# Strassen additions moved from VectorE into TensorE's accumulation, and more TensorE work during the list building, in a masked attention layer on one core

## The chip, the cores and the metric

The kernel runs on one core of a Trainium2 chip. The metric is the device time of one execution in microseconds. The kernel before takes 2042.49 us (median of three runs, 2041.43 to 2042.58). The profile below is of one execution with a span of 2041.5 us and a mean granted TensorE clock of 0.977.

The engines have short names: PE is TensorE (PEld its weight loads), DVE is VectorE, ACT is ScalarE, POOL is GpSimd, SP is SyncE. PSUM, where matmuls write, has eight banks of 128 x 512 float32; SBUF holds everything else.

## The reference

For x of shape (16, 1024, 512) and a sparse 0/1 matrix adj of shape (1024, 1024), with eight heads of 64 and float32 throughout:

```python
q = (x @ Wq + bq).reshape(b, n, H, HD)
k = (x @ Wk + bk).reshape(b, n, H, HD)
v = (x @ Wv + bv).reshape(b, n, H, HD)
scores = einsum('bqhd,bkhd->bhqk', q, k) / sqrt(HD) + (1.0 - adj) * -1e9
out = einsum('bhqk,bkhd->bqhd', softmax(scores), v).reshape(b, n, d)
return layernorm(x + out @ Wo + bo)
```

adj has few ones: the kernel works with a list of neighbours for each query instead of the full score matrix.

## The kernel before, in words

**Lists.** At the start the queries are sorted by their number of neighbours, and `edges(t)` makes, for each of eight tiles of 128 queries, columns of key rows: `OWN` columns with one key for each query of the tile (29 in all), and for the two tiles with the most neighbours `BLOCKS` shared columns (6 in all). So a batch of x has NB = 35 blocks, and 16 batches have 560. The lists are the same for all batches and are made once, mostly by DVE.

**Fronts.** For each batch the rows of x are transposed on PE (`transpose_x`) and multiplied by Wq (`product`, four accumulated matmuls of 128 x 512) and by Wk and Wv. The last two are done together for a pair of row tiles in `pair(b, j)`: the pair's 2 x 2 blocks (two row tiles by two halves of the depth) against the 2 x 2 blocks B11, B21 (Wk) and B12, B22 (Wv) are one Strassen-Winograd product with seven half-depth products where the plain one has eight. The combinations of the weights are T1 to T4, those of x are s1 to s4 (`combine`). Each half-depth product is a `unit` of two matmuls. The results go to `kv_rows` and `q_rows` in HBM. The very first pair is done plainly. Every float32 matmul of the program is two instructions in the trace.

With p1 = x00·B11 in bank x, the kernel before forms the outputs so:

- ACT copies p1 from bank x to an SBUF tile e (`out_e`, L679). PE then adds p2 onto bank x, and ACT copies that out as k of the first row tile (`out_k`, L583).
- DVE adds p6 (its own bank) and e into w (`out_w`, L682), p7 and w into g (`out_g`, L685), and p4 and g into k of the second row tile (`out_k1`, L689).
- p5 goes to bank z; DVE adds z and g into v of the second row tile (`out_v1`, L694). PE adds the last product onto z, and DVE adds z and w into v of the first row tile (`out_v0`, L698).

So there are five DVE additions of 128 x 512 for each of the 63 Strassen pairs.

**Blocks.** For block n, POOL gathers 128 rows of k and v (`gather`, L810), DVE multiplies by q (`products`, L827) and sums over each head (`scores`, L831), ACT takes the exponential (`exponentials`, L841), and the values are multiplied by it (`weigh`). This last can be done by ACT, as eight instructions of 128 x 64 (L851), or by DVE, as one of 128 x 512 (L855); `by_act(n)` chooses. The products are then added by DVE (`add_own`, L867) or, for the shared columns, by PE (`add_up`, L876 and L877). `normalise` divides, PE transposes (`poT`, L902), ACT copies (`oT`, L906), and `finish` does the output projection (`po`, four matmuls), the residual and the layer norm, and POOL scatters the rows out.

**Order.** The program's order is written by hand, and each engine runs its instructions in that order. A loop over steps n goes from -34 (`LEAD_IN`) past 560; a step works on several blocks in turn (scores of n + 4, exponentials of n + 3 and so on). In each step PE also gets units of fronts or of a finish until a `credit` is used up, which grows by `share` a step; a unit is booked at `PRODUCT` = 0.86 for one matmul of 512 columns. Before block 0 the share is `LEAD_SHARE`. At each batch's start the share is set from what is left to a goal. The goal depends on the batch alone, so whatever was done early is taken off the next share. `later(k, fn)` puts the copy that empties a bank k steps on. A Strassen unit may name a result that it needs; while the step that makes it has not been written yet, no further unit is put out.

**Banks.** Four PSUM banks are shared by everything that is emptied soon (`fill_psum`: projections, transposes, p4, p6, p7), x and z have one each, and two hold the sums of the shared columns. A bank can be written again when what is in it has been read.

Of the kernel before, what the change touches and what calls it, by code (L numbers as in the profile page):

```python
# [10 lines left out]
F32 = mybir.dt.float32  # L11
# [3 lines left out]
OP = mybir.AluOpType  # L15
# [9 lines left out]
OWN = (1, 2, 2, 3, 4, 5, 5, 7)  # L25
# [16 lines left out]
LEAD_IN = 34  # L42
# [3 lines left out]
SUM = 0.87  # L46
TRANSPOSE = 0.44
LEAD_SHARE = 3.45
LAST_SHARE = 3.0

P = 128
# [103 lines left out]
def kernel(  # L155
# [35 lines left out]
    nc = tc.nc  # L191
    B, N, D = x.shape
# [3 lines left out]
    HALF = N // 2  # L196
# [25 lines left out]
    with ExitStack() as main:  # L222
# [4 lines left out]
        dram = main.enter_context(tc.tile_pool(name="dram", bufs=1, space=bass.MemoryType.DRAM))  # L227

        def fill_psum(name):
            return psum.tile([P, HALF], F32, tag="fill", name=name, bufs=4)  # L230

        neg_half = one.tile([P, 1], F32, name="neg_half")
        nc.gpsimd.memset(neg_half, -0.5)
# [106 lines left out]
        def later(k, fn):  # L340
            plan.setdefault(now[0] + k, []).append(fn)

        def later_last(k, fn):
            rest.setdefault(now[0] + k, []).append(fn)
# [219 lines left out]
        def pair(b, j):  # L564
# [25 lines left out]
            def send(i):  # L590
                kv = KV[b, tt[i]]
                later(1, lambda: nc.sync.dma_start(kv_rows[b % ROWS][ds(tt[i] * P, P), :], kv))
                R["sent"] = R.get("sent", 0) + 1
                if R["sent"] == 2:
                    later(1, add_v)
                    if j == NT // 2 - 1:
                        later(2, lambda: urgent.append(mean_pe))
# [57 lines left out]
            def a(i, h):  # L655
                return XT[b, tt[i]][:, ts(h, HD2)]

            def unit(bank, left, right, first, after, need):
                def pe():
                    if first:  # L660
                        R[bank] = fill_psum(f"p{bank}_{b}_{j}") if bank[0] == "p" else psum.tile(
                            [P, HALF], F32, tag=bank, name=f"{bank}_{b}_{j}", bufs=1
                        )
                    l = left()
                    for c in range(2):
                        nc.tensor.matmul(  # L666
                            R[bank], l[:, ts(c, P)], right[:, c, :], start=(first and c == 0), stop=(c == 1),
                            skip_group_check=True,
                        )
                    later(1, after)  # L670

                return [(2 * PRODUCT, pe, lambda: (need is None or need in R) and (b, j) in SX)]

            def temp(name):
                R[name] = work.tile([P, D], F32, tag=name, name=f"{name}_{b}_{j}", bufs=1)
                return R[name]

            def out_e():
                nc.scalar.copy(temp("e"), R["x"])  # L679

            def out_w():
                nc.vector.tensor_tensor(temp("w"), R["p6"], R["e"], op=OP.add)  # L682

            def out_g():
                nc.vector.tensor_tensor(temp("g"), R["p7"], R["w"], op=OP.add)  # L685

            def out_k1():
                kv = KV[b, tt[1]]
                nc.vector.tensor_tensor(kv[:, 0:D], R["p4"], R["g"], op=OP.add)  # L689
                send(1)  # L690
                later_last(1, lambda: norm(b, tt[1], 1, kv[:, 0:D]))

            def out_v1():
                nc.vector.tensor_tensor(new_kv(1)[:, D:], R["z"], R["g"], op=OP.add)  # L694
                R["v1"] = True

            def out_v0():
                nc.vector.tensor_tensor(KV[b, tt[0]][:, D:], R["z"], R["w"], op=OP.add)  # L698
# [2 lines left out]
            def s(i):  # L701
                return lambda: SX[b, j][i - 1]

            units = []
            units += unit("x", lambda: a(0, 0), B11, True, out_e, None)
            units += unit("p6", s(2), T2, True, out_w, None)
            units += q0
            units += unit("x", lambda: a(0, 1), B21, False, lambda: out_k(0, R["x"]), "e")
            units += unit("p7", s(3), T3, True, out_g, None)
            units += xt  # L710
            units += unit("z", s(1), T1, True, out_v1, None)
            units += q1
            units += unit("p4", lambda: a(1, 1), T4, True, out_k1, None)
            units += unit("z", s(4), B22, False, out_v0, "v1")
            return units

# [125 lines left out]

        def by_act(n):
            b, t, i = blocks[n]
            return 0 < i < OWN[t] or n % 2 == 0 or n < NB // 2

        def weigh(n):
            v, pv = KG.pop(n), PV[n]
# [108 lines left out]
        out_rows = {(b, t): out_views[b * NT + t].rearrange("b n d -> (b n) d") for b in range(B) for t in range(NT)}  # L957
        done, coming, spilled, gathered, fronts = [], [], [], [0], []

        total = len(blocks)  # L960
        prep = {}
        for t in range(NT):
# [5 lines left out]
        with tc.manual_schedule():  # L968
# [13 lines left out]
            while n < total or plan or rest or urgent or done or finishing or spilled:  # L982
                now[0] = n
                if n < 0:
                    share = LEAD_SHARE if n > -LEAD_IN else TRANSPOSE * 1.5
                elif n >= SPILL[0] // NT * NB + NB:

                    share = sum(u[0] for u in fronts) / max(fronts_end - n, 1) + NS * SUM / NB if fronts else LAST_SHARE
                elif n % NB == 0:

                    left = sum(u[0] for u in fronts)
                    goal = fronts_time - (n // NB + 2 + (EARLY + (FIRST if n < NB else 0)) / NB) * batch_time
                    share = (max(0.0, left - goal) + NT * NPAIR * PRODUCT + NS * SUM) / NB
                if 0 <= n + 3 < total:
                    exponentials(n + 3)
                if 0 <= n + 4 < total:
                    products(n + 4)
                while gathered[0] < min(n + (AHEAD if fronts else AHEAD_LAST) + 1, total) and blocks[gathered[0]][0] in set_up:
                    gather(gathered[0])
                    gathered[0] += 1  # L1000
                if 0 <= n + 1 < total and not by_act(n + 1):
                    weigh(n + 1)
                if 0 <= n < total and blocks[n][2] < OWN[blocks[n][1]]:
                    add_own(n)
                if 0 <= n + 4 < total:
                    scores(n + 4)
                if 1 <= n <= total and (n == total or blocks[n][2] == 0):
                    normalise(*blocks[n - 1][:2])
                for fn in plan.pop(n, ()):
                    fn()  # L1010
                if 0 <= n + 2 < total and by_act(n + 2):
                    weigh(n + 2)
                for fn in rest.pop(n, ()):
                    fn()
                credit += share
                if 0 <= n < total and blocks[n][2] >= OWN[blocks[n][1]]:
                    add_up(n)
                    credit -= SUM
                for tile_done in done[:0 if fronts and len(done) < LAZY else 1 if fronts else 2] + coming:
                    if tile_done not in loaded and sum(b * NT + t not in SPILL for b, t in Y) < 5:  # L1020
                        load_y(*tile_done)
                coming[:] = [t for t in coming if t not in loaded]
                if spilled and not fronts and n > last_reload + 2 and sum(b * NT + t in SPILL for b, t in Y) < 3:
                    reload(*spilled.pop(0), reloads)
                    reloads, last_reload = reloads + 1, n
                first_unit = True
                while credit > 0 or urgent:
                    if urgent and not (first_unit and fronts):
                        urgent.pop(0)()
                        continue  # L1030
                    if not finishing and len(done) > (LAZY if fronts else 0) and n > loaded.get(done[0], n) + 1 and n > last_finish + 1:
                        finishing = finish(*done.pop(0))
                        last_finish = n
                    units = finishing or fronts
                    if not units:
                        if urgent:
                            urgent.pop(0)()
                            continue
                        break
                    cost, fn, ready = units[0]  # L1040
                    if ready and not ready():
                        if urgent:
                            urgent.pop(0)()
                            continue
                        break
                    del units[0]
                    fn()
                    credit -= cost
                    first_unit = False
                credit = min(credit, share)  # L1050
                preps += prep.pop(n, [])
                preps = [g for g in preps if next(g, True) is None]
                n += 1
# [34 lines left out]
```

## Time and profile before

| What | Value |
|---|---|
| Time, median of 3 | 2042.49 us |
| PE busy | 1917.2 us, 94% |
| DVE busy | 1801.0 us, 88% |
| ACT busy | 1684.6 us, 83% |
| POOL busy | 1302.5 us, 64% |
| DMA queue with the largest share | 59.8% of the 16 engines' span |

Busy time is the union of an engine's instructions. Matmuls overlap in the pipeline, so PE's share says when something was in it and not how densely it was fed. The groups of instructions give the line, the engine, the operation, its tiles and shapes, the count, the busy time and the mean of one; then the engine's idle time ahead of them and who ended most of it. The windows give each engine's busy time in a stretch of the span, the granted TensorE clock (1.00 is full) and the share of the DMA engines.

### The profile page before, as it was taken

The numbers are of one execution on the slowest core, as the hardware profiler recorded it, in microseconds if no ns is written. First come the engines' busy times: TensorE is split into PE (matmuls) and PEld (weight loads), VectorE is DVE, ScalarE is ACT, GpSimd is POOL, SyncE is SP. The second block draws the span as 40 slices with busy tenths as digits, with TensorE's granted clock in tenths as the row PEclk, the third lists the DMA queues.
The fourth block names the chain that finished last, engine by engine and source line by source line (L and its number), as shares of the span: only waits on it lengthen the run. The fifth ranks groups of instructions, "written<-read, shape, count | busy, mean of one in ns | idle before, by whom it ended". The sixth has DMA issues, their size and how long they took to land. (4 is left out here: it accounts for less than half of the span.)

```text
span 2041.5 us, 26505 instructions
## 1 busy us (share of the span) xinstructions
PE 1917.2 (94%) x5334; PEld 925.4 (45%) x5334; DVE 1801.0 (88%) x3675; ACT 1684.6 (83%) x7048; POOL 1302.5 (64%) x1224
## 2 busy tenths in 40 slices
PE   8979999899999999999999999999999999997565
PEld 4434454444545444444544444454544444443232
DVE  3798889889999989989999999989999999997684
ACT  4627879888897988889897989879798889987684
POOL 1432557757576666757676676758677675757884
PEclk9999999999999999999999999999999999999897
DMA  6565787878888787878888797888888799978773
GB/s 244 154 202 195 241 297 264 296 237 303 288 295 292 261 307 258 310 242 303 293 287 307 242 327 250 293 283 289 293 271 305 257 321 313 326 255 281 231 253 103
DMA packets 183657, 549.50 MB, mean 269 GB/s; under 512 B 30879, under 2 KB 30907, under 8 KB 183486
## 3 DMA queue, kind: packets, MB, share of 16 engines
q0 software_dynamic: 121632, 403.22, 59.8%
q1 hardware_dynamic: 59248, 139.53, 18.4%
q10 hardware_dynamic: 2606, 4.99, 0.7%
q14 instruction: 127, 1.04, 0.2%
q8 instruction: 44, 0.72, 0.1%
HBM read 435.44 MB, written 136.89 MB: 280 GB/s over the span
## 5 line engine op out<-in xcount | busy, mean ns | idle before, releaser
L810 POOL DMA_INDIRECT kvg<-kv_rows,key_row x560 | 634.9, 1134 | 468.1 <-ACT pv L841 145.1
L851 ACT ACTIVATE pv<-kvg,pv 128x64 f32<-128x64 f32 x3608 | 910.2, 342 | 0.0
L550 PE MATMUL pq<-wq,xT 128*128 128x512 f32 x1024 | 479.7, 599 | 0.2 <-DVE g L685 0.2
L550 PE MATMUL po<-wo,oT 128*128 128x512 f32 x944 | 439.0, 599 | 0.7 <-ACT oT L906 0.7
L831 DVE TENSOR_REDUCE s<-qk 128x8 f32<-128x512 f32 x560 | 381.0, 680 | 6.4
L827 DVE TENSOR_TENSOR qk<-qt,kvg 128x512 f32<-128x512 f32 x464 | 317.4, 684 | 5.9 <-DMA kvg<-kv_rows,key_row 5.8
L550 PEld LDWEIGHTS pq<-wq,xT 128*128 128x128 f32 x1024 | 193.8, 192 | 216.2 <-issue 197.4
L550 PEld LDWEIGHTS po<-wo,oT 128*128 128x128 f32 x944 | 176.5, 192 | 209.2 <-issue 191.8
L666 PE MATMUL x<-b,xT 128*128 128x512 f32 x504 | 239.1, 597 | 0.0
L666 PE MATMUL pp<-t,s 128*128 128x512 f32 x504 | 237.0, 592 | 0.4 <-DVE s L536 0.4
L867 DVE TENSOR_TENSOR pv<-pv,pv 128x520 f32<-128x520 f32 x336 | 233.1, 694 | 0.2 <-ACT pv L851 0.2
L841 ACT ACTIVATE pv<-s,absent 128x8 f32<-128x8 f32 x464 | 136.9, 296 | 85.1 <-DVE s L831 55.8
L767 POOL DMA_INDIRECT out_dram<-y,asked_row x128 | 151.0, 1180 | 35.5 <-issue 16.9
L725 POOL DMA_INDIRECT y<-in_x_dram,asked_row x128 | 143.0, 1117 | 38.9 <-issue 37.7
L562 ACT ACTIVATE sq<-q 128x128 f32<-128x128 f32 x512 | 151.1, 303 | 17.5 <-DVE q L577 17.1
L794 POOL DMA_INDIRECT qt<-q_rows,asked_row x128 | 140.4, 1097 | 38.9 <-issue 34.6
L562 ACT ACTIVATE sq<-kv 128x128 f32<-128x128 f32 x512 | 151.0, 302 | 0.1
L666 PEld LDWEIGHTS x<-b,xT 128*128 128x128 f32 x504 | 95.8, 191 | 116.6 <-issue 111.5
L666 PEld LDWEIGHTS pp<-t,s 128*128 128x128 f32 x504 | 94.8, 190 | 110.6 <-issue 99.2
L902 PE MATMUL poT<-ident,o 128*128 128x128 f32 x512 | 79.5, 279 | 50.2 <-DVE o L894 34.1
L666 PE MATMUL z<-b,s 128*128 128x512 f32 x252 | 120.1, 599 | 5.0 <-DVE kv L694 5.0
L804 POOL DMA_INDIRECT qg<-q_rows,query_row x96 | 106.9, 1114 | 27.8 <-issue 24.1
(168 smaller groups left out, 2816.1 us busy)
## 6 DMA issues: line engine op xcount, KB each, us to landing
kv_rows<-kv SPq DMA_DIRECT2D x128, 512.0 KB
x<-in_x_dram SPq DMA_DIRECT2D x128, 256.0 KB
q_rows<-q SPq DMA_DIRECT2D x128, 256.0 KB
kvg<-kv_rows,key_row POOLq DMA_INDIRECT x560, 5.8
adj<-in_adj_dram POOLq DMA_DIRECT2D x8, 512.0 KB, 12.7
spill<-oT SPq DMA_DIRECT2D x10, 256.0 KB
oTs<-spill SPq DMA_DIRECT2D x10, 256.0 KB
qt<-q_rows,asked_row POOLq DMA_INDIRECT x128, 5.0
```

The costliest lines, as they stand in the source:

```text
L550: nc.tensor.matmul(p, lhs()[:, ts(c, P)], w[:, c, :], start=(c == 0), stop=(c == NPAIR - 1))
L562: nc.scalar.activation(sq, s[:, ts(h, P)], AF.Square, accum_out=NRM[b][:, i, t, h:h + 1])
L666: nc.tensor.matmul(R[bank], l[:, ts(c, P)], right[:, c, :], start=(first and c == 0), stop=(c == 1), skip_group_check=True,)
L725: nc.gpsimd.indirect_dma_start(out=Y[b, t], out_offset=None, in_=x_rows, in_offset=bass.IndirectOffsetOnAxis(ap=asked_row[:, t:t + 1], axi ...
L767: nc.gpsimd.indirect_dma_start(out=out_rows[b, t], out_offset=bass.IndirectOffsetOnAxis(ap=asked_row[:, t:t + 1], axis=0), in_=y, in_offse ...
L794: nc.gpsimd.indirect_dma_start(out=QT[b, t], out_offset=None, in_=q_rows[b % ROWS], in_offset=bass.IndirectOffsetOnAxis(ap=asked_row[:, t: ...
L810: nc.gpsimd.indirect_dma_start(out=KG[n], out_offset=None, in_=kv_rows[b % ROWS], in_offset=bass.IndirectOffsetOnAxis(ap=key_row[:, g:g + ...
L827: nc.vector.tensor_tensor(QK[n], q, KG[n][:, 0:D], op=OP.mult)
L831: nc.vector.tensor_reduce(S[n], QK.pop(n).rearrange("p (h d) -> p h d", d=HD), axis=AX.X, op=OP.add)
L841: nc.scalar.activation(PV[n][:, D:], S.pop(n), AF.Exp, bias=bias)
L851: nc.scalar.activation(pv[:, ts(h, HD)], v[:, ds(D + h * HD, HD)], AF.Copy, scale=pv[:, D + h:D + h + 1])
L867: nc.vector.tensor_tensor(PV[b, t], PV[b, t], pv, op=OP.add)
```

## The change

Three of the five additions go to PE. ACT copies p1 from bank x into a third bank u (a PSUM bank of its own, taken from the shared ones, which are now three). PE adds p6 onto it, and ACT copies the sum out as w. PE adds p7 onto the same bank, and ACT copies that out as g. PE adds p4, and ACT copies that out as k of the second row tile. The two additions with z stay on DVE. So that a matmul can add onto what ACT wrote, one matmul writes bank u at the start.

The units are put in another order: z's first product comes ahead of the transposes of the next pair, and p7 and p4 each wait, in the writing of the program, for the copy out of u (p4 for the addition of g into v one step after that).

Every second of the eligible blocks that ACT weighed goes to DVE: `n % 2` becomes `n % 4`. And from step -15 to step -1, where the lists are made, the share of PE work rises from 3.45 to `LISTS_SHARE` = 4.6.

```diff
+LISTS_SHARE = 4.6
...
-            return psum.tile([P, HALF], F32, tag="fill", name=name, bufs=4)
+            return psum.tile([P, HALF], F32, tag="fill", name=name, bufs=3)
+
+        def chain_psum(name):
+            return psum.tile([P, HALF], F32, tag="u", name=name, bufs=1)
...
             def out_e():
-                nc.scalar.copy(temp("e"), R["x"])
+                R["u"] = chain_psum(f"u_{b}_{j}")
+                nc.scalar.copy(R["u"], R["x"])
 
             def out_w():
-                nc.vector.tensor_tensor(temp("w"), R["p6"], R["e"], op=OP.add)
+                R["w"] = work.tile([P, D], F32, tag="w", name=f"w_{b}_{j}", bufs=1)
+                nc.scalar.copy(R["w"], R["u"])
 
             def out_g():
-                nc.vector.tensor_tensor(temp("g"), R["p7"], R["w"], op=OP.add)
+                R["g"] = work.tile([P, D], F32, tag="g", name=f"g_{b}_{j}", bufs=1)
+                nc.scalar.copy(R["g"], R["u"])
+                later(1, out_v1)
...
-                nc.vector.tensor_tensor(kv[:, 0:D], R["p4"], R["g"], op=OP.add)
+                nc.scalar.copy(kv[:, 0:D], R["u"])
...
             units += unit("x", lambda: a(0, 0), B11, True, out_e, None)
-            units += unit("p6", s(2), T2, True, out_w, None)
             units += q0
-            units += unit("x", lambda: a(0, 1), B21, False, lambda: out_k(0, R["x"]), "e")
-            units += unit("p7", s(3), T3, True, out_g, None)
+            units += unit("u", s(2), T2, False, out_w, "u")
+            units += unit("x", lambda: a(0, 1), B21, False, lambda: out_k(0, R["x"]), "u")
+            units += unit("z", s(1), T1, True, None, None)
             units += xt
-            units += unit("z", s(1), T1, True, out_v1, None)
+            units += unit("u", s(3), T3, False, out_g, "w")
             units += q1
-            units += unit("p4", lambda: a(1, 1), T4, True, out_k1, None)
+            units += unit("u", lambda: a(1, 1), T4, False, out_k1, "v1")
             units += unit("z", s(4), B22, False, out_v0, "v1")
...
-            return 0 < i < OWN[t] or n % 2 == 0 or n < NB // 2
+            return 0 < i < OWN[t] or n % 4 == 0 or n < NB // 2
...
+        nc.tensor.matmul(chain_psum("u_first"), ident, place[:, 0:HALF], start=True, stop=True)
...
-                    share = LEAD_SHARE if n > -LEAD_IN else TRANSPOSE * 1.5
+                    share = LISTS_SHARE if n > -16 else LEAD_SHARE if n > -LEAD_IN else TRANSPOSE * 1.5
```

More of the change, by code (lines that the diff above doesn't have):

```diff
@@ L660, in pe @@
                     if first:
-                        R[bank] = fill_psum(f"p{bank}_{b}_{j}") if bank[0] == "p" else psum.tile(
-                            [P, HALF], F32, tag=bank, name=f"{bank}_{b}_{j}", bufs=1
-                        )
+                        R[bank] = psum.tile([P, HALF], F32, tag=bank, name=f"{bank}_{b}_{j}", bufs=1)
                     l = left()
@@ L669, in pe @@
                         )
-                    later(1, after)
+                    if after:
+                        later(1, after)
                 return [(2 * PRODUCT, pe, lambda: (need is None or need in R) and (b, j) in SX)]
-            def temp(name):
-                R[name] = work.tile([P, D], F32, tag=name, name=f"{name}_{b}_{j}", bufs=1)
-                return R[name]
             def out_e():
-                nc.scalar.copy(temp("e"), R["x"])
+                R["u"] = chain_psum(f"u_{b}_{j}")
+                nc.scalar.copy(R["u"], R["x"])
             def out_w():
-                nc.vector.tensor_tensor(temp("w"), R["p6"], R["e"], op=OP.add)
+                R["w"] = work.tile([P, D], F32, tag="w", name=f"w_{b}_{j}", bufs=1)
+                nc.scalar.copy(R["w"], R["u"])
             def out_g():
-                nc.vector.tensor_tensor(temp("g"), R["p7"], R["w"], op=OP.add)
-            def out_k1():
-                kv = KV[b, tt[1]]
-                nc.vector.tensor_tensor(kv[:, 0:D], R["p4"], R["g"], op=OP.add)
-                send(1)
-                later_last(1, lambda: norm(b, tt[1], 1, kv[:, 0:D]))
+                R["g"] = work.tile([P, D], F32, tag="g", name=f"g_{b}_{j}", bufs=1)
+                nc.scalar.copy(R["g"], R["u"])
+                later(1, out_v1)
             def out_v1():
@@ L695, in out_v1, with out_k1 @@
                 R["v1"] = True
+            def out_k1():
+                kv = KV[b, tt[1]]
+                nc.scalar.copy(kv[:, 0:D], R["u"])
+                send(1)
+                later_last(1, lambda: norm(b, tt[1], 1, kv[:, 0:D]))
             def out_v0():
```

## The prediction

> **What bounds the kernel now.** I read the totals first, then the 40 slices, then the windows of six stages, because the stages here have different limits. From the page, the totals and four rows of slices (51 us each):
>
> ```profile
> PE 1917.2 (94%) x5334; PEld 925.4 (45%) x5334; DVE 1801.0 (88%) x3675; ACT 1684.6 (83%) x7048; POOL 1302.5 (64%) x1224
> ...
> PE   8979999899999999999999999999999999997565
> ...
> DVE  3798889889999989989999999989999999997684
> ACT  4627879888897988889897989879798889987684
> ...
> PEclk9999999999999999999999999999999999999897
> ```
>
> Busy PE need not be dense PE. The PE timeline settles it; start, length, and how many matmuls:
>
> ```profile
> 1011.20 3.60 PE L550 MATMUL pq<-wq,xT 128*128 128x512 f32 x8
> 1014.63 1.88 PE L666 MATMUL x<-b,xT 128*128 128x512 f32 x4
> ```
>
> Eight matmuls take 1014.63 - 1011.20 = 3.43 us, 0.429 each from start to start. A batch needs 240 of them (8 tiles x 8 for q, 8 x 8 for the output projection, 4 pairs x 28), so 103.0 us. Add 64 transposes at 0.109 (7.0), 24 matmuls of the shared sums at 0.22 (5.3) and two for the mean (0.9): 116.2 us. The matmul of the mean (L610) stands at 606.8 in one batch and 723.3 in the next, 116.5 us apart. In the middle PE has no gap at all.
>
> The windows (PE, PEld, DVE, ACT, POOL, then clock, DMA share, GB/s):
>
> ```profile
> 90.00:180.00 90.00, 71.55 (x180) 32.66 (x179) 86.93 (x190) 35.87 (x168) 25.02 (x25) 0.91 0.54 178
> 180.00:285.00 105.00, 104.96 (x291) 49.49 (x291) 88.74 (x174) 87.68 (x386) 59.85 (x55) 1.00 0.77 261
> 315.00:375.00 60.00, 51.66 (x147) 23.72 (x146) 58.94 (x128) 58.32 (x239) 44.87 (x44) 1.00 0.84 284
> 450.00:1650.00 1200.00, 1198.78 (x3392) 582.50 (x3391) 1113.94 (x2263) 1060.62 (x4499) 823.28 (x755) 1.00 0.83 285
> 1695.00:1770.00 75.00, 71.25 (x204) 33.44 (x203) 74.23 (x134) 75.00 (x345) 46.90 (x38) 1.00 0.92 320
> 1860.00:2010.00 150.00, 93.57 (x226) 44.23 (x225) 114.80 (x278) 109.86 (x393) 119.44 (x123) 0.85 0.73 238
> ```
>
> The lists (90 to 180) are DVE's: 97% busy, with PE idle for 18 us and at a lower clock. The rest of batch 0 (180 to 285) is PE's. Batch 1 (315 to 375) is held by DVE at 98% and ACT at 97% together, since its PE share is small. The middle is PE's. Around 1695 to 1770 ACT never rests. In the tail POOL is 80% busy with gathers about 0.3 us apart and no other engine is above 77%.
>
> **What the skill says.** Trainium Kernel Development and Optimization, section Performance Expectations, calls matmul busy time a bad metric of nearness to the roofline and prefers the share of weight loads. The trace agrees on the first (busy 3.60 us for 3.43 of spacing); on the second it shows 45% PEld in a stretch without gaps, so I go by spacing. PSUM — Partial Sum Buffer, The four PSUM rules, says that a matmul without the starting flag adds onto what another engine wrote where an earlier matmul has set the bits: that is what the one matmul on u is for, and it means the three additions cost PE nothing; no run here shows it yet. TensorE: Matmul & The Clock Gate, Step-by-step: what each phase is for, says only weight loads are pulled ahead and matmuls stay in program order, so a matmul that waits for ACT holds all PE work. The waits of before agree: PE sat still in front of poT for DVE's o for 34.1 us while other units stood behind it.
>
> **The change, part by part.** The rows for it:
>
> ```profile
> L851 ACT ACTIVATE pv<-kvg,pv 128x64 f32<-128x64 f32 x3608 | 910.2, 342 | 0.0
> ...
> L855 DVE TENSOR_TENSOR pv<-kvg,pv 128x512 f32<-128x512 f32 x109 | 74.7, 686 | 0.0
> ...
> L685 DVE TENSOR_TENSOR g<-pp,w 128x512 f32<-128x512 f32 x63 | 43.2, 686 | 17.2 <-PE pp L666 16.8
> ...
> L679 ACT COPY e<-x 128x512 f32<-128x512 f32 x63 | 36.6, 581 | 77.8 <-PE x L666 77.8
> ```
>
> *PE.* Two instructions more, under 1 us, while PE waits for its first data. Its 5334 instructions stay, so the middle can't get shorter.
>
> *DVE and ACT.* Three additions fewer for each of 63 pairs: 189 x 0.685 = 129 us off DVE. Three copies more on ACT: 189 x 0.58 = 110 us. The copy into u goes to PSUM, which no row shows; the nearest row is the copy to SBUF at 0.581, and ScalarE: Activation LUTs, What ACT_TABLE_LOAD costs, prices an ACTIVATE without pointer operands at 186 + 0.833 x 512 = 612 ns (estimate). I take 0.58; the difference over 63 is 2 us. The rule n % 4 moves 56 blocks: 448 ACT instructions of 910.2 / 3608 = 0.252 us, so -113 us, and 56 x 0.686 = +38 us for DVE. Totals: DVE -91, ACT -3. A middle batch has DVE 5.8 us lighter and ACT level (12 x 0.58 = 7.0 against 3.5 x 2.02 = 7.1). All hidden behind PE there.
>
> *The share of the lists.* Fifteen steps get 1.15 more, 17.25 us of PE work, and the planner takes it off batch 0. A pair is 19.8 us of PE and costs DVE 7.9 us now (two q, five additions, four halves of s, two of the mean) and 5.85 after. The lists hold about 2.65 pairs: DVE -5.4 for the additions, +5.1 for the 0.87 pair moved in. So DVE's bound there stays 90 us, and PE's 71.6 rises to about 89 of 90, tight. Batch 0's PE falls from 105 to 88 us; DVE there comes to about 77 and ACT to about 80, so PE still ends last. Gain 17 us at most; I allow 3 us for a tight lists stretch where PE and DVE wait for each other: **-14**.
>
> *Batch 1*, held by DVE and ACT: 2.4 pairs x 2.05 off DVE, 3.5 x 0.69 on; ACT +4.2 and -7.1. Both about -3: **-3**. *1695 to 1770*, held by ACT, which is level: **-1**. *Tail*, held by POOL: **0**.
>
> *New waits in the middle.* In the built order of the changed program I looked at how much PE work lies between the matmul that an ACT or DVE instruction waits for and the matmul that waits for that instruction. Along the u chain it is 3.4 us at least from p1 to p6, 4.3 from p6 to p7 and 3.4 from p7 to p4, with medians of 6.4, 8.2 and 7.3. In the trace of before, ACT has emptied x into e 0.62 us after p1's end in the median, 2.9 in the slowest tenth, 3.15 at most. So the chain itself seldom stops PE. The three shared banks do: in nine batches the second transpose of xT at the batch's end needs the bank of poT, whose copy waits for the end of a po, and only 0.44 us of PE work lies between. In the old order no such distance is under 2.15 us. Copy 0.62 + lateness of ACT (mean 1.2 - 0.62) + 0.05 - 0.44 gives 0.8 us each. In eight batches a q product then waits for DVE's y 2.6 us after po ended; y is done after 2.2 us on average, so about 0.3. Together about 1 us a batch: **+9**; 4 if ACT is always early, 25 if the new copies, 12 a batch that each tie ACT to PE, eat ACT's 13 us of slack a batch (1200 - 1060.62 over 10.3 batches). Behind a late copy on ACT stand the exponentials and the weighing, and for those waits the shared sums on PE.
>
> Sum: -14 - 3 - 1 + 9 = -9, so 2042.5 - 9 = **2033.5 us**.
>
> **Rivals.** *More relief:* PE and DVE fit together in the lists (-18), batch 1 gains on both engines (-6), 1695 to 1770 is eased (-4), the bank waits are short (+2): 2016. For it speaks that DVE's lateness should fall with its load; against it that ACT, not DVE, never rests at 1700. *Evened out:* the bank waits cost 1.75 us a batch (+19) and lists and batch 1 give -18: 2043. For it speaks that y is over 4 us late in a tenth of cases. *Slower:* ACT becomes late. 24 synchronised copies a batch become 36, and PE loses 3.5 us a batch over 10.3 batches, +36 - 18: 2060. For it speaks ACT's 88% and that e already had to wait 77.8 us for PE, time that ACT can't use ahead; against it that ACT's total work doesn't rise.
>
> **How the numbers follow.** Likeliest case 0.53, more relief 0.16, evened out 0.15, slower 0.16. Faster by over 0.2% (below 2038.4) holds the first two: 0.69; same 0.15; slower 0.16. The range from 2013 to 2055 holds the first three cases and the near edge of the last.
>
> **What would show it.** Right: PE idle in 90 to 180 falls from 18 us to under 8, block 35's scores (281.0 before) come 10 to 17 us sooner, ACT has 7048 - 259 and DVE 3675 - 133 instructions, and the middle shows a PE gap of about 1 us once a batch in front of pxT with ACT's oT as its end. Wrong: a middle batch of over 118.5 us with PE waiting on u for ACT (the slower case), or a lists stretch that grows by as much as batch 0 shrinks.

## The result and the profile after

The changed kernel takes 2062.07 us (median of four runs, 2061.34 to 2063.54) beside 2041.96 us for the kernel before in the same comparison: ratio 1.010, 95% interval 1.0083 to 1.0118. It is slower by 20 us where the forecast was 9 us faster.

From the page of the changed kernel, the totals and three rows of slices:

```profile
PE 1930.3 (94%) x5336; PEld 924.0 (45%) x5336; DVE 1722.1 (84%) x3542; ACT 1674.6 (81%) x6789; POOL 1300.9 (63%) x1224
...
PE   8999999899999999999999999999999999997765
...
DVE  3699898888887988898898988898898889896775
ACT  4639989697897979788897989789797979787674
```

DVE has 3675 - 133 and ACT 7048 - 259 instructions, and their busy times fell by 79 and 10 us. The work moved as intended: the engines that were relieved are idler, and the program is longer.

The windows of the stages shown before, of the changed kernel (PE, PEld, DVE, ACT, POOL, clock, DMA share, GB/s):

```profile
90.00:180.00 90.00, 82.53 (x229) 38.12 (x228) 86.79 (x190) 49.75 (x221) 26.57 (x25) 0.98 0.55 195
180.00:285.00 105.00, 103.33 (x294) 50.16 (x293) 90.59 (x180) 92.02 (x388) 64.52 (x60) 1.00 0.84 282
315.00:375.00 60.00, 54.05 (x134) 24.72 (x133) 54.29 (x116) 53.98 (x219) 45.92 (x45) 0.91 0.85 286
450.00:1650.00 1200.00, 1183.82 (x3338) 571.21 (x3337) 1038.21 (x2124) 1036.38 (x4261) 800.48 (x739) 1.00 0.82 279
1695.00:1770.00 75.00, 70.06 (x208) 33.44 (x206) 68.47 (x125) 72.06 (x318) 39.19 (x33) 0.98 0.86 296
1860.00:2010.00 150.00, 102.00 (x232) 46.24 (x230) 110.74 (x262) 105.45 (x388) 118.03 (x119) 0.85 0.76 248
```

In the lists PE's idle time fell from 18.4 to 7.5 us. In the middle, where PE had 1.2 us of idle time in 1200 us, it now has 16.2, and runs 3338 matmul instructions where it ran 3392. DVE does less there mostly because work was taken from it; ACT, which has as much to do in a batch as before, does less because the whole program moves slower.

Where the time went is read best from the start of the scores of a block (in the trace, by counting L831 before and L834 after), since a block is the same piece of work in both. The times run from the start of the span, as in the windows; the 281.0 us of the prediction for block 35 is counted from the first busy instruction, 0.26 us later.

| Block | before, us | after, us | after - before | of it in this stretch |
|---|---|---|---|---|
| 0 | 140.3 | 142.7 | +2.4 | +2.4 |
| 35 | 281.3 | 268.4 | -12.9 | -15.3 |
| 70 | 389.3 | 374.5 | -14.8 | -1.9 |
| 420 | 1555.6 | 1565.8 | +10.2 | +25.1 |
| 490 | 1772.9 | 1787.9 | +15.1 | +4.8 |
| 525 | 1893.4 | 1914.0 | +20.6 | +5.5 |
| end | 2041.5 | 2060.5 | +19.0 | -1.6 |

So the early gain is there, and the ten batches from block 70 to block 420 lose 2.5 us each in the mean, the first of them 5. What PE waited for between 450 and 1650 us, the seven longest lines of the changed kernel (us in total, times, longest):

```profile
PE po L554 <- ACT xT L529: 4.0, 4, 2.5
PE u L668 <- ACT u L679: 2.9, 2, 1.8
PE pq L554 <- DVE y L746: 2.8, 2, 1.8
PE pxT L525 <- ACT oT L909: 2.2, 8, 0.5
PE pq L554 <- ACT xT L529: 1.4, 2, 0.8
PE z L668 <- DVE kv L691: 1.3, 2, 0.7
PE po L554 <- ACT oT L909: 1.1, 2, 0.6
```

The kernel before has one line between 435 and 1672 us:

```profile
PE poT L902 <- ACT xT L525: 1.2, 1, 1.2
```

A po or pq does not use xT or oT of that moment; it waits for the copy that empties the shared bank it is about to write. The lines with xT, oT and y as the end are such waits, 11.5 us here. Those with u and z, 4.2 us, are the chain's.

Does this account for the loss? The 54 instructions that are missing from the window are about 19 us of PE's work, at 1200 / 3392 = 0.354 us each. The added idle time is 15 us of it. A lower clock after one stop adds 1.6 us (last section), and some 3 us stay unexplained.

One of the waits for xT in the timeline of the changed kernel (start, length, what):

```profile
455.95 1.04 PE L525 MATMUL pxT<-ident,x 128*128 128x128 f32 x8
...
458.54 1.02 PE L554 MATMUL pq<-wq,xT 128*128 128x512 f32 x2
...
461.48 1.05 ACT L529 COPY xT<-pxT 128x512 f32<-128x512 f32 x2
...
462.11 1.22 PE L554 MATMUL po<-wo,oT 128*128 128x512 f32 x1 [2.55 <-ACT xT L529]
```

PE had transposed x by 456.99. ACT, which did not rest between 455 and 465, came to copy it out at 461.48. In its order PE had no other work left ahead of the po that wanted that bank, so it stood for 2.55 us.

### The profile page after: what moved, and what is told of

Read it like the earlier page. It is cut to its first block, busy times and chain, and to the rows that moved or that the text cites. A ratio compares the mean times of both kernels' runs of the same rounds, so it can differ in the third digit from the quotient of the medians.

```text
span 2060.5 us, 25998 instructions
## 1 busy us (share of the span) xinstructions
PE 1930.3 (94%) x5336; PEld 924.0 (45%) x5336; DVE 1722.1 (84%) x3542; ACT 1674.6 (81%) x6789; POOL 1300.9 (63%) x1224
## 3 DMA queue, kind: packets, MB, share of 16 engines
q14 instruction: 124, 1.02, 0.1%
## 5 line engine op out<-in xcount | busy, mean ns | idle before, releaser
L813 POOL DMA_INDIRECT kvg<-kv_rows,key_row x560 | 642.1, 1147 | 493.3 <-ACT pv L854 177.4
L854 ACT ACTIVATE pv<-kvg,pv 128x64 f32<-128x64 f32 x3160 | 798.1, 343 | 0.0
L554 PE MATMUL po<-wo,oT 128*128 128x512 f32 x944 | 448.8, 610 | 12.1 <-ACT xT L529 5.9
L834 DVE TENSOR_REDUCE s<-qk 128x8 f32<-128x512 f32 x560 | 380.8, 680 | 5.3
L668 PE MATMUL u<-t,s 128*128 128x512 f32 x504 | 237.2, 593 | 2.9 <-ACT u L679 2.9
L770 POOL DMA_INDIRECT out_dram<-y,asked_row x128 | 145.1, 1134 | 39.5 <-issue 18.8
L668 PEld LDWEIGHTS u<-t,s 128*128 128x128 f32 x504 | 90.6, 190 | 91.0 <-issue 82.7
L668 PE MATMUL u<-t,xT 128*128 128x512 f32 x252 | 120.3, 600 | 5.4 <-ACT g L687 5.4
L746 DVE TENSOR_TENSOR y<-po,y 128x512 f32<-128x512 f32 x128 | 87.8, 686 | 43.9 <-PE po L554 43.5
```

The costliest lines, as they stand in the source:

```text
L554: nc.tensor.matmul(p, lhs()[:, ts(c, P)], w[:, c, :], start=(c == 0), stop=(c == NPAIR - 1))
L668: nc.tensor.matmul(R[bank], l[:, ts(c, P)], right[:, c, :], start=(first and c == 0), stop=(c == 1), skip_group_check=True,)
L770: nc.gpsimd.indirect_dma_start(out=out_rows[b, t], out_offset=bass.IndirectOffsetOnAxis(ap=asked_row[:, t:t + 1], axis=0), in_=y, in_offse ...
L813: nc.gpsimd.indirect_dma_start(out=KG[n], out_offset=None, in_=kv_rows[b % ROWS], in_offset=bass.IndirectOffsetOnAxis(ap=key_row[:, g:g + ...
L834: nc.vector.tensor_reduce(S[n], QK.pop(n).rearrange("p (h d) -> p h d", d=HD), axis=AX.X, op=OP.add)
L854: nc.scalar.activation(pv[:, ts(h, HD)], v[:, ds(D + h * HD, HD)], AF.Copy, scale=pv[:, D + h:D + h + 1])
```

## The experiments

The kernel before took 2047.56, 2055.5 and 2053.69 us in the three groups of runs that follow, so kernels are compared by their ratio to the before of their own group.

| Run | Ratio | 95% interval |
|---|---|---|
| larger list share alone, on the kernel before | 0.9928 | 0.9903 to 0.9953 |
| changed kernel, sums in one bank, three shared banks | 1.0076 | 1.0050 to 1.0102 |
| the same with four shared banks | 0.9936 | 0.9911 to 0.9962 |
| kernel before with three shared banks | 1.0257 | 1.0231 to 1.0284 |
| changed kernel, old list share | 1.0152 | 1.0121 to 1.0184 |
| changed kernel, old rule n % 2 | 1.0136 | 1.0101 to 1.0171 |
| new rule alone, on the kernel before | 0.9983 | 0.9970 to 0.9996 |
| chain in bank x, four shared banks | 0.9863 | 0.9834 to 0.9892 |
| changed kernel, units in another order | 1.0288 | 1.0243 to 1.0333 |
| chain in bank x, three shared banks | 1.0026 | 1.0014 to 1.0038 |
| chain in bank x, old rule n % 2 | 0.9943 | 0.9921 to 0.9965 |
| changed kernel once more | 1.0071 | 1.0044 to 1.0097 |

**Is the early gain the share's?** Theory: the larger share alone makes it. Rival: it needs the DVE that the chain set free.

```diff
-                    share = LEAD_SHARE if n > -LEAD_IN else TRANSPOSE * 1.5
+                    share = LISTS_SHARE if n > -16 else LEAD_SHARE if n > -LEAD_IN else TRANSPOSE * 1.5
```

> The kernel before with only the larger share of PE work in the list steps (4.6 in place of 3.45). If the early gain comes from the share alone: block 35's scores come 10 to 15 us sooner and the time is about 2030, since the middle keeps its four shared banks and loses nothing. If the gain needs the lighter DVE of the chain in bank u: the lists are bound by DVE, so the work moved in costs it 0.87 x 7.9 = 7 us there, the lists stretch grows by that, and the time is 2035 to 2042.

It measured 2033.5 us beside 2047.56, 14 us less, the size of the first theory's gain. Block 35 comes at 271.7 us: 9.6 us sooner than before and 3.4 us later than in the changed kernel. Most of the early gain is the share's; a few microseconds may be the chain's. The same edit undone in the changed kernel:

```diff
-LISTS_SHARE = 4.6
+LISTS_SHARE = 3.45
```

> The changed kernel with the old share of 3.45 in the list steps; chain in bank u, three shared banks and the new rule stay. Theory of the banks with an early gain from the share: the early gain of 13 us goes and the middle's loss stays, so about 2075, 1.6% over the kernel before. If the chain's lighter DVE were what shortens the lists: it keeps 5 us or more of the early gain, 2065 to 2070.

It is 1.5% over the kernel before, as the first theory said, and block 35 comes at 284.2 us, 3 us later than in the kernel before. So the chain together with the loss of its bank shortens nothing at the start. That is not the chain by itself: in the kernel before with only three shared banks (a run below) block 35 comes at 289.8 us. At the same number of banks, chain, order and rule together are some 5 us ahead, in one trace of each.

**Banks or chain?** The change ties PE to ACT in two ways: through bank u, and through the bank that u took from the shared ones. To give the bank back without undoing the chain, the shared sums go into one bank by one matmul of 512 columns, and the denominators of the shared columns are left out. The control has the same sums and three shared banks:

```diff
-            nc.tensor.matmul(PSUM[b, t][:, 0, 0:HD2], m, pv[:, 0:HD2], **kw)
-            nc.tensor.matmul(PSUM[b, t][:, 1, 0:HD2 + HEADS], m, pv[:, HD2:], **kw)
+            nc.tensor.matmul(PSUM[b, t], m, pv[:, 0:D], **kw)
```

> Control for the next run. The changed kernel with the shared sums done by one matmul of 512 columns in one bank in place of 256 and 264 in two; the sums of the shared columns' denominators are left out. The bank set free is not used: three shared banks as in the changed kernel. All theories: within 5 us of the changed kernel, about 2060.

> As the control, denominators of the shared columns left out, but with four shared banks beside bank u. Theory of the banks (the middle loses its 2.5 us a batch mainly because PE waits for shared banks that ACT and DVE have not emptied): 15 to 20 us less than the control, about 2043, and the PE gaps with xT, oT and y as their end vanish from the middle. Theory of the chain (PE waits for ACT's copies in and out of u, and ACT is tied to PE): at most 6 us less than the control, with a middle batch still near 118 us.

The control took 2064.61 us, the four-bank version 2035.15: 29 us less, more than the 15 to 20 that I expected. All of PE's waits from 450 to 1650 us in the four-bank version:

```profile
PE u L668 <- ACT u L679: 2.9, 2, 1.8
PE poT L901 <- DVE o L893: 0.7, 1, 0.7
PE z L668 <- issue: 0.7, 1, 0.7
PE z L668 <- DVE s L541: 0.7, 1, 0.7
PE sum L879 <- DVE pv L858: 0.6, 1, 0.6
```

Every wait for xT, oT and y is gone and the one for u is unchanged to the tenth. The two profiled executions differ by 36.5 us, somewhat more than the medians: 14 before block 105 (3 of them before block 35), 15 from there to block 420 (1071.4 and 1056.4 us for these nine batches) and 7 after it. So the missing bank cost time in the early batches too. The reverse edit in the kernel before:

```diff
-            return psum.tile([P, HALF], F32, tag="fill", name=name, bufs=4)
+            return psum.tile([P, HALF], F32, tag="fill", name=name, bufs=3)
```

> The kernel before with three shared banks in place of four and one bank left unused, nothing else. Theory of the banks: slower, by 25 us or more, since p4, p6 and p7 still use the shared banks (eleven users a pair where the changed kernel has eight). Theory of the chain: the number of shared banks hardly matters, under 8 us slower.

54 us slower, with neither chain nor copies in it.

**Number of banks, or distance?** In the built order of each program I counted, over the middle, the PE instructions that wait for an ACT or DVE instruction which itself waits for a matmul less than 2.5 us of PE work earlier. I call this a short tie; the counts depend by one or two on where the middle is taken to begin and end: 1 in the kernel before, 14 in the changed one, 0 with one-bank sums and four shared banks, 45 in the kernel before with three. Another order of the units changes this count and not the number of banks:

```diff
-            units += xt
             units += unit("u", s(3), T3, False, out_g, "w")
-            units += q1
+            units += xt + q1[0:3]
             units += unit("u", lambda: a(1, 1), T4, False, out_k1, "v1")
+            units += q1[3:]
             units += unit("z", s(4), B22, False, out_v0, "v1")
```

> The changed kernel with another order of a pair's units and nothing else: the third u product comes before the next pair's transposes, which share a stretch with three quarters of the second q product. Three shared banks. In the built order, between blocks 70 and 420 or so, 35 PE instructions wait for an ACT or DVE instruction that itself waits for a matmul less than 2.5 us of PE work earlier (14 in the changed kernel, 1 in the one before). If those short ties set the loss: slower than the changed kernel by 5 to 20 us, 1.3 to 2.0% over the kernel before. If only the number of banks counts: equal to the changed kernel, 1.0%.

1.0288 against 1.0071 for the changed kernel on the same chip: 44 us for an order, beyond even the range expected of the short ties. The longest of its waits of PE from 450 to 1650:

```profile
PE po L554 <- ACT xT L529: 17.9, 12, 3.0
PE pq L554 <- ACT xT L529: 13.6, 5, 4.5
PE pq L554 <- ACT oT L909: 5.9, 4, 1.8
PE pq L554 <- DVE y L746: 3.8, 4, 2.2
```

The same kinds of waits as in the changed kernel, four times as long. So at the same number of banks the distances alone can cost as much as a bank does; a bank more is one way to lengthen them. The count of short ties is only a rough sign of the loss. In the changed kernel they stand in front of pxT, where PE waited 2.5 us in all; none of its waits for xT, 5.4 us, belongs to a tie under 2.5 us. How late the copy is must be known too.

> The changed kernel itself, on the same chip as the other three of this group, for the comparisons: 1.0% over the kernel before.

**The rule.** Two runs, each with the one number changed (n % 4 to n % 2 in the changed kernel, n % 2 to n % 4 in the kernel before):

> The changed kernel with the old rule n % 2: ACT keeps all the blocks it weighed and gets the chain's copies on top, 113 us more for ACT and 38 less for DVE than in the changed kernel. Theory of the banks: ACT goes from 86% to about 92% in the middle and empties shared banks later, so the waits for xT and oT grow: 10 to 25 us slower than the changed kernel. If ACT's lateness has no part in it: within 5 us of the changed kernel.

> The kernel before with only the new rule n % 4: 56 blocks weighed by DVE in place of ACT, four shared banks, no chain. Theory of the banks: the middle is PE's and has no waits for banks, so DVE's 38 us more are hidden there; batch 1 and the stretch around 1700, held by DVE and ACT, may change by some us each: 2038 to 2052. If DVE's load is what counts: slower by 20 us or more.

Without the rule the changed kernel is at 1.0136, against 1.0100 and 1.0071 with it: 0.4 to 0.7% slower, by point estimates whose intervals touch or nearly do. PE's idle time from 450 to 1650 is 27.3 us, where the two traces of the changed kernel have 16.2 and 20.9. This is what the theory of the banks says of a busier ACT, but the difference in time is hardly clear of the scatter. On the kernel before the rule is worth 0.2%: DVE's 38 us are hidden.

**A chain without a bank of its own.** p6, p7 and p4 can be added in bank x, onto p1 itself, if ACT first copies p1 out and p2 goes elsewhere:

```diff
+            def out_k0():
+                kv = new_kv(0)
+                nc.vector.tensor_tensor(kv[:, 0:D], R["p2"], R["e"], op=OP.add)
...
+            units += unit("p2", lambda: a(0, 1), B21, True, out_k0, "e")
+            units += unit("z", s(1), T1, True, None, None)
+            units += unit("x", s(2), T2, False, out_w, "e")
+            units += q0
+            units += unit("x", s(3), T3, False, out_g, "w")
+            units += xt + q1[0:3]
+            units += unit("x", lambda: a(1, 1), T4, False, out_k1, "v1")
+            units += q1[3:]
             units += unit("z", s(4), B22, False, out_v0, "v1")
```

> The chain without a bank of its own: p6, p7 and p4 are added in bank x itself, onto p1, after ACT has copied p1, w and g out of it; p2 goes to a shared bank and DVE adds it to the copy of p1. So there are three DVE additions a pair in place of five (two in the changed kernel), four shared banks with nine users a pair, the larger list share, the rule n % 4, and no copy into PSUM. Theory of the banks: the middle returns to 116.5 us a batch and the early gain of 13 us or more stays: about 2027, and below both kernels. Theory of the chain (PE tied to ACT's copies): a middle batch stays at 118 us or more, since bank x has four such ties a pair: 2050 or more.

2026.31 us, 0.9863 of the kernel before: faster than both, by 1.4% and, over the ratios, 2 to 2.4%. Its windows of the lists and of the middle:

```profile
90.00:180.00 90.00, 80.80 (x224) 37.27 (x223) 87.20 (x185) 45.53 (x209) 26.05 (x24) 0.96 0.57 189
...
450.00:1650.00 1200.00, 1198.08 (x3392) 581.49 (x3391) 1078.38 (x2203) 1030.81 (x4287) 825.03 (x749) 1.00 0.84 284
```

The middle is dense again, with the 3392 matmuls of the kernel before, though PE is tied to ACT four times a pair through bank x. Two or three ties in the middle are under 2.5 us. Some 100 are under 4 us, mostly those through bank x; but ACT is earlier here: xT is copied 1.8 us after its transposes end in the mean and 3.4 in the slowest tenth (2.8 and 5.5 in the kernel before). Against the larger share alone it is 0.65% better. Two variants of it:

> The chain in bank x with three shared banks in place of four, one bank unused. 30 ties under 2.5 us where four banks have 2. Theory of the banks: 30 to 60 us over the version with four banks, so slower than the kernel before by 0.5 to 1.6%. If that version's gain comes from the chain's lighter work for DVE and ACT: within 10 us of it, still faster than the kernel before.

> The chain in bank x with four shared banks and the old rule n % 2: 113 us more for ACT, 38 less for DVE. With four banks the middle is PE's and hides it, so the loss is confined to batch 1 and the stretch around 1700, where ACT never rests: 0 to 10 us over the version with n % 4. If ACT's lateness matters in the middle as with three banks, where the same edit cost 0.4%: 8 to 20 us over it.

With three shared banks it loses 1.6% and is slower than the kernel before: without the fourth bank its gain is gone. With the old rule it loses 0.8%, some 16 us, outside the 0 to 10 that I wrote for the theory of the banks. At 0.9943 it is then no better than the larger share alone (0.9928). So the chain shows no gain here without the rule that takes work off ACT. The larger share with that rule and without the chain was not run (the two ratios alone give 0.9928 x 0.9983 = 0.991), so what the chain itself adds to the 0.9863 is not shown.

Where the 0.8% is lost is not settled. The batches from 105 to 420 take 1060.1 us where n % 4 takes 1053.5, and between 450 and 1650 us PE waits three times for ACT's copy w, which it never does with n % 4:

```profile
PE x L667 <- ACT w L687: 3.9, 3, 2.1
```

That speaks for ACT's load in the middle. But the kernel before and the one with the larger share alone, which have the same four banks and the same order of units, differ by more there: 1049.8 and 1057.2 us.

## Why the prediction was wrong

**Right.** The lists: -14 was forecast, and block 35 came 12.9 us sooner. The counts of instructions, and PE idle in the lists under 8 us (7.5). The three additions cost PE nothing: 5336 instructions, two more. ACT's copy into PSUM took 0.579 us where 0.58 was taken from the SBUF copy, and 0.612 was the skill's price (ScalarE: Activation LUTs, What ACT_TABLE_LOAD costs). DVE's relief did make it earlier: y is done 1.5 us after po in the mean over the middle, where it was 2.0. Batch 1, with -3 forecast and -1.9 measured, is right in part by luck: in the version with four shared banks it gains 3.8 us, so the missing bank took back half.

**The step that failed** is "New waits in the middle", with its sum "Together about 1 us a batch: +9". It measured 2.5 us a batch, +25 to block 420, and another +10 from there to block 525, for which the prediction had -1. The mechanism was named and only partly counted:

- Waits for oT: nine of 0.8 us, 7 us, in the sum. They came to 2.2 us in front of pxT and 1.1 in front of po.
- Waits for y: about 2.4 us in the sum, 2.8 us in front of pq.
- Waits for xT: no term. They came to 5.4 us in front of po and pq.
- The chain: "seldom stops PE", so nothing. Its waits with u and z came to 4.2 us.
- What a stop costs beyond its length: no term. It was 1.6 us once in the middle (last section).

The term for xT is missing because I looked for ties shorter than 2.15 us, the shortest in the old order, and priced ACT's lateness by its copy of x into e, which is done 0.62 us after the matmul in the median and 1.2 in the mean. The copies that empty the shared banks are later ones: in the trace of before, xT is copied 2.8 us after its transposes end in the mean and 5.5 us in the slowest tenth, oT 2.8 and 4.3. Against those, ties of 2.5 to 4 us can stop PE as well. By my count the changed order has some 65 ties under 4 us where the old has under 30, and in 18 of them a po or pq waits for xT, where the old order has one. The trace of before had the lateness; I took it from the wrong row. The number of such ties does not give the loss by itself: the chain in bank x has some 100 and loses nothing, with xT copied earlier.

**Readings and signs.** Two readings of the kernel before were rough: the 45% of weight loads is that of the whole span, and the stretch almost without gaps has 49% (582.5 of 1200 us); and PE had one gap of 1.2 us in the middle. A middle batch took 118.9 us (1069.8 us for the nine from block 105 to 420), over the 118.5 that was to speak for the slower case; but its other half, PE waiting on u for ACT, came to 2.9 us in 1200.

**The rivals.** "Slower" gave 2060 us, 2 us off, and for a reason that the runs don't bear out, so its number was luck. It had ACT late through 36 synchronised copies a batch in place of 24. ACT is no later in the changed kernel (xT 2.8 us before and 2.9 after, oT 2.8 and 2.9), and with all 36 copies and one bank more the time is that of the larger share alone (0.9936 and 0.9928). "Evened out", 2043 us, was nearest in mechanism, with bank waits of 1.75 us a batch, and too small in size. After the middle the chain may have a larger part: from block 420 to 525 the changed kernel takes 348.2 us, the four-bank version 341.0 and the kernel before 337.9. In the first two, u waits there three times for ACT's copy g, 5.4 and 5.5 us. So 7 of the 10 us lost there go with the bank. The other 3 are not settled: the new rule alone, with four banks and no chain, takes 345.0 us there.

What the Trainium skill states in TensorE: Matmul & The Clock Gate, Step-by-step, that matmuls stay in program order, agrees: the po at 462.11 held all PE work behind it for 2.55 us.

## What to carry to other kernels

Where one engine is dense, moving work off the others can gain nothing there (the kernel before and the chain in bank x both run 3392 matmul instructions in 1200 us), and a resource taken from it can cost time at once: here one of four shared PSUM banks cost 54 us in the kernel before and 29 us in a version of the changed one. Before a buffer is taken away, list how much work lies between its last use and its next, in the program's own order, and hold that against how late the emptying engine is for that very copy, at its slowest tenth and not at its median. Adding in a bank that is already there relieved DVE here without the loss of a bank. It was faster than the larger share alone only together with the rule that took work off ACT.

## What the runs showed of the hardware

A stop of PE can cost more than its length. PE stood for 2.55 us until 462.1, and the granted clock was half from 461.8 for 3.4 us; after a stop of 3.47 us that ended at 1748.35 it was half for 3.4 us again. Windows of the changed kernel (columns as above; the clock is the third number from the end):

```profile
460.00:465.00 5.00, 2.90 (x4) 1.35 (x5) 2.98 (x7) 5.00 (x19) 3.78 (x5) 0.68 0.92 322
...
1745.00:1750.00 5.00, 1.65 (x2) 0.63 (x3) 4.58 (x10) 5.00 (x25) 1.49 (x1) 0.86 0.50 156
```

After the stop that ended at 462.1 the next matmuls started 1.02, 0.85, 0.85 and 0.61 us after the one before, where 0.43 is the spacing at full clock: about 1.6 us on top of the stop. After the other, four matmuls took 3.57 us, where four took 1.88 at full clock.

The length of the stop alone does not decide this. A stop of 1.23 us in the kernel before, at 761, did not bring it: the next record of a lower clock in that trace comes at 1866 us. But in the changed kernel with the other order of units a stop of 3.43 us that ended at 1500.0 left the clock full, while one of 2.21 us that ended at 1170.1 was followed by half clock:

```profile
1170.00:1174.50 4.50, 4.41 (x7) 1.88 (x8) 4.40 (x12) 4.50 (x19) 1.77 (x3) 0.62 0.59 204
...
1500.00:1504.00 4.00, 3.99 (x10) 1.84 (x11) 1.52 (x4) 3.03 (x11) 1.56 (x2) 1.00 0.55 190
```

What decides is not shown by these runs.
